# Global attention: split rows stored once, the first rows of maxima sent from ScalarE's queue, projections spread, tails by ScalarE and GpSimd, first local input early

## The chip, the cores and the metric

The kernel runs on one core of one Trainium2 chip. The metric is the device time of one execution in microseconds; lower is better. The kernel before took 2326.94 us in the median of three runs (2325.54 to 2329.14). Engine names in the profile: PE is TensorE (PEld its weight loads), DVE is VectorE, ACT is ScalarE, POOL is GpSimd, SP is SyncE, which here only issues DMAs (SPq is its queue).

## The reference

The input x is 1 x 2048 x 128 in fp32. It is normalised once (xn), and two things are computed from xn and added to x:

```python
xn = _layernorm(x)
x = x + attn(xn, Wq, bq, Wk, bk, Wv, bv, Wo, bo, U, V) + ffn_stack(xn, ...)

# attn: 16 heads of 8 numbers (V and U are 8 x 8), full softmax over 2048 keys
zq, zk, zv = q @ V, k @ V, v @ V
att = softmax(einsum('bhqr,bhkr->bhqk', zq, zk) / sqrt(8))
y = einsum('bhqk,bhkr->bhqr', att, zv) @ U.T ; return y @ Wo.T + bo

# ffn_stack: 6 layers, 16 heads of 64, windows of 32 tokens that look one window back
for i in range(6):
    x = local_attention_layer(shift_tokens(x)) + x     # q, k normalised, rotary tables
    x = ffn_layer(shift_tokens(x)) + x                 # layernorm, gated gelu
```

## The kernel before, in words

The program has two parts that run one after the other: the global attention (class `GlobalAttention`, about 0 to 697 us) and the six local layers (class `LocalStack`, from 697 us to the end). The second needs nothing of the first but xn, transposed, which lies in `xa`.

**Global attention.** A score needs more precision than one pass of the multiplier has, so queries and keys are split in a head (hi, the number rounded to the multiplier's format) and a tail (lo, what is left), and a score is the sum of three products: hi*hi, lo*hi, hi*lo. This is laid out along the contraction: a head's stack of queries has 8 rows each of hi, lo, hi, its stack of keys 8 rows each of hi, hi, lo, and row 24 (`ROWS`) holds a one on the keys' side and, on the queries' side, minus the maximum of the query's scores. Each stack stands twice in SBUF, on partitions 0 to 24 and 64 to 88, and matmuls use the two copies in turn (`half`, line 235). Two buffers of each stack alternate between heads (`qs[h % 2]`, `ks[h % 2]`).

For head 0 the stacks are computed directly (`first_stack`, line 145). For the others, `project` (line 202) computes 512 columns of all heads' queries or keys, ACT writes the head (line 209), DVE the tail (line 210), and `store_rows` (line 220) writes three pieces of 8 rows per head into a DRAM tensor `rows` of 25 rows per head. `load_stack` (line 228) later loads a head's 25 rows, with one DMA for each copy of each stack, in the middle of the head before.

The work of a head is four steps: "M" (`max_step`, line 241) computes 128 queries by 1024 keys on PE and reduces them to a maximum on DVE, 64 of them per head; "T" (`finish_max`, line 258) transposes the four maxima of a 512-query block, ACT negates them (`nm`, line 263) and two DMAs put them as row 24 into both copies of the query stack (line 266); "E" (`exp_step`, line 268) computes keys by queries again, with the maximum now subtracted by row 24, and ACT takes the exponential, 64 per head; "V" (`value_step`, line 277) multiplies by the values. The order is written out by hand in `STEPS` (line 59): a round has 8 M, 1 T, 16 E and 8 V, E runs 26 and V 17 steps behind. T comes after a round's second M; the first E that needs this T's maxima is the eleventh E of the round, right after the fifth M. `load_stack` for the next head stands at the head's 21st M. Before this, the steps M 0 to 2 carry the rest of `first_stack`, M 3 to 10 the eight projections and stores, M 11 to 14 the values (lines 370 to 377). From the 100th M on, each round also takes one step of `first_weights` of the local layers (line 482), which loads and splits the first layer's weights.

The order on each engine and in each DMA queue is the program's, under `manual_schedule`, except in the first stretch (lines 315 to 347), where only POOL's order is fixed. All DMAs of the program go through SP's queue. A DMA takes the next of eight completion semaphores and waits at its issue until the DMA before it on that semaphore has landed.

**Local layers.** 48 steps of 256 tokens run as a software pipeline: `ORDER` (line 390) lists all operations of a round with a lag each, and round n runs operation o for step n - lag (line 1097). What the change touches: `xh` and `xl` (lines 562, 565) split the input in head and tail, `tabq` and `tabk` (549, 552) load rotary tables, `tk` (555) scales them on ACT; `k` (588) projects keys, `k2` and `k1` (602, 597) multiply them by the tables on DVE, `ka` (608) adds on POOL. `xl` also clears the three `vbd` tiles on POOL in its first call (lines 570 to 573); `buffers` (519) clears `kbd` on DVE.

Of the kernel before, what the change touches and what calls it, by code (L numbers as in the profile page):

```python
# [8 lines left out]
F32 = mybir.dt.float32  # L9
F32R = mybir.dt.float32r  # L10
AF = mybir.ActivationFunctionType
ALU = mybir.AluOpType
# [4 lines left out]
T = 2048  # L17
# [44 lines left out]
class GlobalAttention:  # L62
# [139 lines left out]
    def project(self, n, b):  # L202
        nc = self.nc
        cols = bass.ts(b, 512)
        zh, zl = self.zsp[n] = [self.zs.tile([128, 512], F32R, tag=n + a, name=f"{n}_{a}") for a in "hl"]
        bz = self.bz[:, "qk".index(n) : "qk".index(n) + 1]
        ps = self.ps_st.tile([128, 512], F32, tag="st", name="ps_z")
        nc.tensor.matmul(ps, self.prod[n], self.xn_T[:, cols], start=True, stop=True)
        nc.scalar.activation(zh, ps, AF.Identity, bias=bz)
        nc.vector.scalar_tensor_tensor(zl, ps, bz, zh.bitcast(F32), ALU.add, ALU.subtract)  # L210

    def values_in(self, b):
        nc = self.nc
# [6 lines left out]
    def store_rows(self, n, b):  # L220

        cols = bass.ts(b, 512)
        for j, part in enumerate((0, 1, 0) if n == "q" else (0, 0, 1)):
            self.nc.sync.dma_start(
                out=self.rows[n][:, 8 * j : 8 * j + 8, cols], in_=self.zsp[n][part].bitcast(F32)
            )

    def load_stack(self, n, h):
        st = (self.qs if n == "q" else self.ks)[h % 2]
        for r in range(2):  # L230
            self.nc.sync.dma_start(
                out=st[64 * r : 64 * r + self.ROWS + 1, :].bitcast(F32), in_=self.rows[n][h]
            )

    def half(self, h):

# [21 lines left out]
    def finish_max(self, h, qb):  # L258
        nc = self.nc
        mt = self.ps_st.tile([128, 512], F32, tag="st", name="mt")  # L260
        nc.tensor.transpose(mt[0:4, 0:128], self.m, self.c["ident"])
        nm = self.sm.tile([4, 128], F32R, tag="nm", name="nm")
        nc.scalar.activation(nm, mt[0:4, 0:128], AF.Copy, scale=-1.0)
        for r in range(2):
            row = self.qs[h % 2][64 * r + self.ROWS : 64 * r + self.ROWS + 1, bass.ts(qb, 512)]
            nc.sync.dma_start(out=row.rearrange("o (a b) -> o a b", a=4).bitcast(F32), in_=nm.bitcast(F32))

    def exp_step(self, h, qb, kb):
        nc = self.nc
# [40 lines left out]
    def run(self):  # L310
        nc = self.nc
        self.zsp, self.mrow, self.pts, self.yp = {}, {}, {}, {}
        self.turns = 0
        self.rows = {n: self.dz.tile([NH, self.ROWS + 1, T], F32, name=f"rows_{n}") for n in "qk"}
        with self.tc.manual_schedule(engines={mybir.EngineType.Pool}):
            self.y = self.ps_y.tile([128, 512], F32, name="y")
            nc.vector.memset(self.y, 0.0)
            for b in range(2):
                self.norm(b)
            ones = self.w.tile([128, 256], F32, name="ones")  # L320
            nc.gpsimd.memset(ones, 1.0)
            zeros = self.w.tile([128, 256], F32, name="zeros")
            nc.gpsimd.memset(zeros, 0.0)
            self.qs = [self.stk.tile([128, T], F32R, name=f"qs{i}") for i in range(2)]
            self.ks = [self.stk.tile([128, T], F32R, name=f"ks{i}") for i in range(2)]
            for a in (self.qs[1], self.ks[1]):
                nc.gpsimd.memset(a.bitcast(F32), 0.0)
            self.zv = self.zp.tile([128, 16, NH, 9], F32, name="zv")

            for n, v in (("q", zeros), ("k", ones)):  # L330
                row = self.rows[n][:, self.ROWS, :]
# [12 lines left out]
            nc.gpsimd.memset(self.zv[:, :, :, 8:9], 1.0)  # L344
            for b in range(4):
                self.layer_input(b)
            self.output_bias()
        with self.tc.manual_schedule():
            self.steps()

    def steps(self):

        count = {"M": 0, "T": -1, "E": -26, "V": -17}
        size = {"M": 8, "T": 1, "E": 16, "V": 8}
        while count["V"] < 4 * 8 * NH:
            if count["M"] > 100:
                next(self.side, None)
            for o in STEPS:
                n = count[o]
                count[o] += 1  # L360
                qb, i = divmod(n, size[o])
                if not 0 <= qb < 4 * NH:
                    continue
                h, qb = divmod(qb, 4)
                if o == "M":
                    if (qb, i) == (2, 4) and h + 1 < NH:
                        self.load_stack("k", h + 1)
                        self.load_stack("q", h + 1)
                    self.max_step(h, 4 * qb + i // 2, i % 2)
                    if n < 3:  # L370
                        self.first_stack("q", n + 1)
                    elif n < 11:
                        z, b = "qk"[n % 2], (n - 3) // 2
                        self.project(z, b)
                        self.store_rows(z, b)
                    elif n < 15:
                        self.values_in(n - 11)
                elif o == "T":
                    self.finish_max(h, qb)
                    if qb == 3 and h:  # L380
                        self.sum_parts(h - 1)
                elif o == "E":
                    self.exp_step(h, qb, i)
                else:
                    self.value_step(h, qb, *divmod(i, 2))
                    if i == 7:
                        self.finish_exp(h, qb)


ORDER = """  # L390
    S.2@3 oh.2@4 pp.0@3 ptk@2 q2.3@2 k.0@1 O.3@4 tk@1 rk@2 wo.2@4 q1.3@2 sub.1@3 wt.qkv.1@2 wd.qkv.0@0 PT.0@3 ot.3@4
# [14 lines left out]
class LocalStack:  # L406
# [15 lines left out]
    def __init__(self, tc, ctx, io, const, xa, yd, out):  # L422
        self.tc, self.nc, self.io, self.c = tc, tc.nc, io, const
        self.xa, self.yd, self.out = xa, yd, out
        self.wl = {}
        self.pj = self.pT = None
        self.st = {}
        self.pw = ctx.enter_context(tc.tile_pool(name="b_w", bufs=1))
        self.pr = ctx.enter_context(tc.tile_pool(name="b_raw", bufs=1))
        self.free = {"raw": [0, 1], "pj": [0, 1, 2], "pt": [0, 1]}  # L430
        self.users = {}

# [49 lines left out]
    def first_weights(self):  # L482
        self.vectors(0)
        for kind, i in (("wo", 0), ("wo", 1), ("w2", 0)):
            self.w_whole((kind, 0, i), f"{kind}{i}", self.w_src(0, kind, i))
            yield
        for kind, i in [("qkv", g) for g in range(NG)] + [("w1", 0)]:
            self.w_load((kind, 0, i), self.w_src(0, kind, i))
            yield
            self.w_head((kind, 0, i), f"{kind}{i}")  # L490
            yield
            self.w_tail((kind, 0, i), f"{kind}{i}")
            yield

    def next_weights(step):
        def method(self, L, s, kind, i=0):
# [22 lines left out]
    def buffers(self, ctx):  # L519
# [16 lines left out]
        for t in self.kbd:  # L536
            for j in range(2):
                nc.vector.memset(t[64 * j : 64 * j + 64, :, :, 1 - j, :], 0.0)
        self.vturn = 0

    def tile(self, key, shape, bufs=1, dt=F32):
        self.st[key] = self.pb.tile(shape, dt, tag=key[0], name=key[0], bufs=bufs)
        return self.st[key]

    def vec(self, L, i):
# [19 lines left out]
    def xl(self, L, s):  # L565
        xh = self.st["xhead", L, s]
        self.nc.gpsimd.tensor_tensor(
            self.tile(("xtail", L, s), [128, TS], 2, F32R), self.xa[:, s * TS : (s + 1) * TS], xh.bitcast(F32), ALU.subtract
        )
        if (L, s) == (0, 0):  # L570
            for t in self.vbd:
                for j in range(2):
                    self.nc.gpsimd.memset(t[64 * j : 64 * j + 64, :, 1 - j, :], 0.0)


    def qk(self, L, s, g, t):
# [513 lines left out]
    def run(self):  # L1090
# [147 lines left out]
```

## Time and profile before

| what | us |
|---|---|
| median of 3 runs | 2326.94 |
| the profiled execution, its time | 2331.27 |
| its span, first to last instruction | 2329.2 |
| DVE's last step before local work (L256) | 680.19 |
| one round of global attention (between L256s) | 9.95 |
| PE busy / DVE busy / ACT busy in the span | 2200.6 / 2031.9 / 1725.1 |
| PE busy / DVE busy / ACT busy from 100 to 150 us | 50.00 / 48.10 / 46.45 |

The profile shows one execution. For each engine a row gives busy time; a group of instructions gives the source line, the engine, the operation, what is written from what, the count, the busy time, the mean time of one in ns, and the idle time of the engine before them with what ended it. The clock that PE was granted is shown as a share of the full one, and the DMA share is the mean busy share of the core's 16 DMA engines.

### The profile page before, as it was taken

To read this page: it belongs to the slowest core of one execution; us is meant where nothing else is said; L and a number is where in the kernel's file an instruction comes from. 1 tells how busy PE (TensorE), PEld (TensorE's weight loads), DVE (VectorE), ACT (ScalarE), POOL (GpSimd) and SP (SyncE) were. 2 spreads that over 40 slices of the span, in tenths; PEclk is the share of its full clock that TensorE was granted. 3 is DMA by queue.
4 is the path that set the end of the run, shared out by engine and by line. 5 is a ranking of instruction groups with operands and counts; after the bars stand their busy time and mean duration, and the time that the engine had idled before them with its cause. 6 is when DMAs were issued, how large, how long until landed. Compare 5 with 4: busy or idle time off the path is not lost.

```text
span 2329.2 us, 69662 instructions
## 1 busy us (share of the span) xinstructions
PE 2200.6 (94%) x27556; PEld 1612.0 (69%) x27556; DVE 2031.9 (87%) x3181; ACT 1725.1 (74%) x3333; POOL 1326.6 (57%) x1216
## 2 busy tenths in 40 slices
PE   6999999999996999999999999999899999999987
PEld 3444444444445888888888888888788878888875
DVE  7999999999975899888888888888799889898885
ACT  4999999999984667777677767676577767777654
POOL 2000100000006788878798778877698778878782
PEclk9999999999999999999999999999999999999998
DMA  4112121111115777877778878787687868777773
GB/s 140 52 60 80 62 69 62 53 63 53 62 47 158 211 215 218 224 223 202 215 220 221 226 205 218 205 225 210 176 229 214 217 189 230 219 216 217 205 214 82
DMA packets 295079, 384.69 MB, mean 165 GB/s; under 512 B 37256, under 2 KB 227464, under 8 KB 293256
## 3 DMA queue, kind: packets, MB, share of 16 engines
q1 hardware_dynamic: 294756, 380.25, 58.2%
q8 instruction: 220, 3.60, 0.7%
q14 instruction: 103, 0.84, 0.1%
HBM read 195.29 MB, written 77.59 MB: 117 GB/s over the span
## 4 chain that ended last, share of the span: by engine, by line
PE 57%; DMA 18%; SPq 9%; DVE 6%; POOL 4%; issue 3%; ACT 3%; POOLq 0%; DVEq 0%; ACTq 0%
PE y L282 11%; PE st L272 9%; PE s L248 6%; PE S L799 6%; DMA rd<-rkt 5%; DMA ur<-t2q 5%; PE ps_o L857 4%; PE ps_q L583 4%; PE ps_n L696 3%; SPq L787 3%; PE ps_wo L885 3%; PE pt_p L835 3%; DMA rbt<-rd 2%; SPq L636 2%; PE ps_v L659 2%
## 5 line engine op out<-in xcount | busy, mean ns | idle before, releaser
L251 DVE TENSOR_REDUCE m<-s 128x1 f32<-128x1024 f32 x512 | 602.2, 1219 | 30.7 <-PE s L248 24.0
L274 ACT ACTIVATE p<-st 128x512 f32<-128x512 f32 x1024 | 542.3, 598 | 44.0 <-PE st L272 13.7
L302 POOL TENSOR_TENSOR z<-z 72x512 f32<-72x512 f32 x15 | 19.2, 1281 | 590.0 <-DMA z<-yp 590.0
L640 POOL TENSOR_TENSOR t1q<-t1q,ur 128x512 f32<-128x512 f32 x192 | 244.7, 1285 | 158.9 <-DMA ur<-t2q 119.2
L282 PE MATMUL y<-p,zv 128*9 128x256 f32 x4096 | 293.1, 381 | 1.5 <-ACT ysb L292 1.5
L248 PE MATMUL s<-ks,qs 64*128 64x512 f32 x1024 | 280.3, 446 | 3.4 <-DVE m L251 1.9
L272 PE MATMUL st<-qs,ks 64*128 64x512 f32 x1024 | 273.0, 434 | 3.8 <-DMA qs<-nm 3.8
L819 POOL TENSOR_TENSOR P<-P,m 128x512 f32<-128x512 f32 x192 | 201.1, 1047 | 103.4 <-DVE m L815 102.8
L610 POOL TENSOR_TENSOR keys<-keys,t2k 128x512 f32<-128x512 f32 x192 | 247.9, 1291 | 5.8 <-DVE keys L599 5.4
L779 POOL TENSOR_TENSOR keys<-keys,rbt 128x512 f32<-128x512 f32 x192 | 243.7, 1294 | 7.2 <-DMA rbt<-rd 6.9
L857 PE MATMUL ps_o<-vbd,PTt 128*32 128x128 f32 x6144 | 210.4, 277 | 16.0 <-DMA vbd<-vd 14.1
L799 PE MATMUL S<-kbd,t1q 128*32 128x128 f32 x6144 | 211.7, 276 | 5.3 <-DMA kbd<-keys 4.5
L272 PEld LDWEIGHTS st<-qs,ks 64*128 64x128 f32 x1024 | 139.8, 184 | 110.5 <-ACT p L274 87.7
L823 POOL TENSOR_TENSOR P<-P,r 128x512 f32<-128x512 f32 x192 | 203.3, 1059 | 7.2
L624 DVE SCALAR_TENSOR_TENSOR t2q<-ps_q,vec,tabq 128x512 f32<-128x512 f32 x192 | 143.0, 745 | 73.7 <-DMA ur<-t2q 56.9
L799 PEld LDWEIGHTS S<-kbd,t1q 128*32 128x32 f32 x6144 | 174.0, 111 | 39.7 <-issue 12.6
L857 PEld LDWEIGHTS ps_o<-vbd,PTt 128*32 128x32 f32 x6144 | 157.8, 110 | 62.9 <-issue 38.5
L885 PE MATMUL ps_wo<-OT,w 128*128 128x256 f32 x768 | 198.7, 382 | 0.7 <-ACT OT L877 0.7
L644 ACT ACTIVATE sq<-ps_k 128x512 f32<-128x512 f32 x192 | 114.1, 595 | 109.3 <-PE ps_k L583 106.7
L248 PEld LDWEIGHTS s<-ks,qs 64*128 64x128 f32 x1024 | 120.9, 184 | 95.7 <-issue 82.3
L282 PEld LDWEIGHTS y<-p,zv 128*9 128x9 f32 x4096 | 74.4, 89 | 148.4 <-issue 96.2
L827 ACT ACTIVATE P<-P 128x512 f32<-128x512 f32 x192 | 121.6, 634 | 64.6 <-POOL P L823 63.8
(201 smaller groups left out, 5825.8 us busy)
## 6 DMA issues: line engine op xcount, KB each, us to landing
vbd<-vd SPq DMA_DIRECT2D x384, 256.0 KB
kbd<-keys SPq DMA_DIRECT2D x768, 72.0 KB
ur<-t2q SPq DMA_DIRECT2D x384, 128.0 KB
vd<-vn SPq DMA_DIRECT2D x96, 512.0 KB
rbt<-rd SPq DMA_DIRECT2D x192, 128.0 KB
tabk<-in_rope SPq DMA_DIRECT2D x48, 384.0 KB
yp<-ysb SPq DMA_DIRECT2D x64, 256.0 KB
tabq<-in_rope SPq DMA_DIRECT2D x48, 256.0 KB
```

The lines of the kernel that those rows point to most:

```text
L248: nc.tensor.matmul(s[:, j, :], q[:, bass.ts(qt, 128)], k[:, bass.ts(2 * hf + j, 512)], start=True, stop=True)
L251: nc.vector.tensor_reduce(self.mrow[h, qt // 4][:, qt % 4, hf : hf + 1], s.rearrange("p a b -> p (a b)"), AX.X, ALU.max)
L272: nc.tensor.matmul(st, k[:, bass.ts(kb, 128)], q[:, bass.ts(qb, 512)], start=True, stop=True)
L274: nc.scalar.activation(p, st, AF.Exp, scale=float(1.0 / 8.0**0.5))
L282: self.nc.tensor.matmul(self.y[32 * c : 32 * c + 9, cols], self.zv[:, kb, h, :], self.pts[h, qb, kb][:, cols], start=(j == 0 and half == 0 ...
L610: self.nc.gpsimd.tensor_tensor(t, t, self.st["t2k", L, s, g], ALU.add)
L640: self.nc.gpsimd.tensor_tensor(t, t, self.st["ur", L, s, g // 2][:, g % 2], ALU.add)
L779: self.nc.gpsimd.tensor_tensor(t, t, bmid(self.st["rbt", L, s][:, g, :], 2), ALU.mult)
L799: self.nc.tensor.matmul(S[32 * w : 32 * w + 32, 4 * i + 2 * p : 4 * i + 2 * p + 2, :], q[:, p, 32 * W : 32 * W + 32], kbd[:, p, :, 32 * W ...
L823: self.nc.gpsimd.tensor_tensor(P4, P4, bc(self.st["r", L, s][:, 0:2, g, :], 64), ALU.mult)
L857: self.nc.tensor.matmul(ps[32 * w : 32 * w + 32, i, p, :, :], PT[:, i, p, 32 * w : 32 * w + 32], vbd[:, w, :, c : c + 64], start=True, sto ...
L885: self.nc.tensor.matmul(self.st["acc", L, s], w[:, 2 * (g % 2) + c, :], o[:, c, :], start=(g == 0 and c == 0), stop=(g == 3 and c == 1),)
```

## The change

- `store_rows` stores each part once: `rows` has 17 rows per head, [lo, hi, row of zeros] for queries and [hi, lo, row of ones] for keys. `load_stack` builds the 25 rows of a stack from two pieces: 16 and 9 rows for queries, 8 and 17 rows for keys. So 8 DMAs load a head in place of 4.
- In `project` ACT writes the sum in fp32 once more (`z`), and POOL subtracts the head from it; DVE's line 210 is gone.
- The first six projections stay at M 3 to 8, two steps of values come at M 9 and 10, the last two projections at M 11 and 12, the last values at M 13 and 14. Keys come ahead of queries as before.
- For head 0 the two DMAs of `nm` are issued by ACT's queue, for the other heads by SP's.
- The clearing of `qs[1]` and `ks[1]` on POOL stands behind the copies into `xa`.
- `tabq`, `tabk`, `xh`, `tk`, `xl` of the first local step run as the last five steps of `first_weights`, one per round of global attention, and are left out where they stood; their tiles have a pool of their own that exists from the start. `vbd` is cleared in `buffers`.

```diff
     def project(self, n, b):
-        nc.vector.scalar_tensor_tensor(zl, ps, bz, zh.bitcast(F32), ALU.add, ALU.subtract)
+        z = self.zs.tile([128, 512], F32, tag="ft", name="z")
+        nc.scalar.activation(z, ps, AF.Identity, bias=bz)
+        nc.gpsimd.tensor_tensor(zl, z, zh.bitcast(F32), ALU.subtract)
...
     def store_rows(self, n, b):
-        for j, part in enumerate((0, 1, 0) if n == "q" else (0, 0, 1)):
-            self.nc.sync.dma_start(
-                out=self.rows[n][:, 8 * j : 8 * j + 8, cols], in_=self.zsp[n][part].bitcast(F32)
-            )
+        for part in range(2):
+            at = 8 * (1 - part if n == "q" else part)
+            self.nc.sync.dma_start(out=self.rows[n][:, at : at + 8, cols], in_=self.zsp[n][part].bitcast(F32))
 
     def load_stack(self, n, h):
-        st = (self.qs if n == "q" else self.ks)[h % 2]
+        st, rows = (self.qs if n == "q" else self.ks)[h % 2], self.rows[n][h]
         for r in range(2):
-            self.nc.sync.dma_start(
-                out=st[64 * r : 64 * r + self.ROWS + 1, :].bitcast(F32), in_=self.rows[n][h]
-            )
+            for to, size, src in ((0, 16, 0), (16, 9, 8)) if n == "q" else ((0, 8, 0), (8, 17, 0)):
+                lo = 64 * r + to
+                self.nc.sync.dma_start(out=st[lo : lo + size, :].bitcast(F32), in_=rows[src : src + size])
...
-            nc.sync.dma_start(out=row.rearrange("o (a b) -> o a b", a=4).bitcast(F32), in_=nm.bitcast(F32))
+            (nc.sync if h else nc.scalar).dma_start(out=row.rearrange("o (a b) -> o a b", a=4).bitcast(F32), in_=nm.bitcast(F32))
...
-        self.rows = {n: self.dz.tile([NH, self.ROWS + 1, T], F32, name=f"rows_{n}") for n in "qk"}
+        self.rows = {n: self.dz.tile([NH, 17, T], F32, name=f"rows_{n}") for n in "qk"}
...
-            for a in (self.qs[1], self.ks[1]):
-                nc.gpsimd.memset(a.bitcast(F32), 0.0)
...
             for b in range(4):
                 self.layer_input(b)
+            for a in (self.qs[1], self.ks[1]):
+                nc.gpsimd.memset(a.bitcast(F32), 0.0)
...
-                    elif n < 11:
-                        z, b = "qk"[n % 2], (n - 3) // 2
+                    elif n < 9 or n in (11, 12):
+                        i = n - 3 if n < 9 else n - 5
+                        z, b = "kq"[i % 2], i // 2
                         self.project(z, b)
                         self.store_rows(z, b)
                     elif n < 15:
-                        self.values_in(n - 11)
+                        self.values_in(n - 9 if n < 11 else n - 11)
...
+EARLY = ("tabq", "tabk", "xh", "tk", "xl")
...
+        self.pe = ctx.enter_context(tc.tile_pool(name="b_early", bufs=1, reuse_waits="tile"))
...
             self.w_tail((kind, 0, i), f"{kind}{i}")
             yield
+        for step in EARLY:
+            getattr(self, step)(0, 0)
+            yield
...
+        for t in self.vbd:
+            for j in range(2):
+                nc.gpsimd.memset(t[64 * j : 64 * j + 64, :, 1 - j, :], 0.0)
         self.vturn = 0
 
     def tile(self, key, shape, bufs=1, dt=F32):
-        self.st[key] = self.pb.tile(shape, dt, tag=key[0], name=key[0], bufs=bufs)
+        pool = self.pe if key[0] in ("tabq", "tabk", "tks", "xhead", "xtail") else self.pb
+        self.st[key] = pool.tile(shape, dt, tag=key[0], name=key[0], bufs=bufs)
...
-        if (L, s) == (0, 0):
-            for t in self.vbd:
-                for j in range(2):
-                    self.nc.gpsimd.memset(t[64 * j : 64 * j + 64, :, 1 - j, :], 0.0)
...
-                    if 0 <= n - lag < DEPTH * NS:
+                    if 0 <= n - lag < DEPTH * NS and (n > lag or step.__name__ not in EARLY):
                         step(*divmod(n - lag, NS), *args)
```

More of the change, by code (lines that the diff above doesn't have):

```diff
@@ L325, in run @@
             self.ks = [self.stk.tile([128, T], F32R, name=f"ks{i}") for i in range(2)]
-            for a in (self.qs[1], self.ks[1]):
-                nc.gpsimd.memset(a.bitcast(F32), 0.0)
             self.zv = self.zp.tile([128, 16, NH, 9], F32, name="zv")
             for n, v in (("q", zeros), ("k", ones)):
-                row = self.rows[n][:, self.ROWS, :]
+                row = self.rows[n][:, 16, :]
                 nc.sync.dma_start(out=row.rearrange("h (a b) -> h a b", a=8), in_=v)
```

## The prediction

> **What bounds the kernel now.** I read the page first (shares of the engines, 40 slices, groups), then the timeline at the three places that the change touches, the chain of waits there, and last the DMA traffic in small windows. In global attention DVE and ACT are nearly full beside a full PE:
>
> ```profile
> L251 DVE TENSOR_REDUCE m<-s 128x1 f32<-128x1024 f32 x512 | 602.2, 1219 | 30.7 <-PE s L248 24.0
> L274 ACT ACTIVATE p<-st 128x512 f32<-128x512 f32 x1024 | 542.3, 598 | 44.0 <-PE st L272 13.7
> ```
>
> A round is 9.95 us (from L256 to L256 on DVE's timeline), and PE is busy for all of 100 to 150 us. So what stops PE in a round is lost for good. Five rounds that hold one ACT cast of 0.84 us (L459) last 10.31: ACT has 0.84 - 0.36 = 0.48 us to spare in a round.
>
> The start (timeline): a POOL memset of a stack holds up a DVE instruction that elsewhere takes 0.15 us.
>
> ```profile
> 9.27 1.82 POOL L327 MEMSET ks<- 128x2048 f32 x1
> 9.29 1.83 DVE L177 TENSOR_SCALAR mu<-mu 128x4 f32<-128x4 f32 x1
> ```
>
> The first exponential (timeline): the maxima are ready at 46.6, their DMAs leave SP's queue at 51.7, behind stores, and PE stands 3.8 us.
>
> ```profile
> 46.33 0.25 ACT L263 ACTIVATE nm<-mt 4x128 fp32r<-4x128 f32 x1
> ...
> 51.71 1.47 SPq L266 DMA_DIRECT2D qs<-nm  x2
> ...
> 54.60 0.46 PE L272 MATMUL st<-qs,ks 64*128 64x512 f32 x1 [3.80 <-DMA qs<-nm]
> ```
>
> The join of the two parts (chain of waits): from 697.3 the chain is the table's load, its scaling, then DVE's first keys.
>
> ```profile
> 697.31 3.65 DMA tabk<-in_rope
> ...
> 703.50 0.69 DVE keys L599
> ```
>
> **The change part by part.** *Start.* DVE's four instructions at 9.29 to 11.2 would take about 0.6 us; the DMAs of x and the products of weights stay. I take -1.3 (0 to -2.0). Behind the copies into xa (about 25 to 29 us) the memsets meet DVE instructions that read PSUM; those kept 0.75 us beside POOL's copies at 22.4 to 25.6, so nothing; without that cover up to 1.8 each.
>
> *Warm-up.* DVE loses eight L210 of 0.75. ACT gets eight more of 0.69, POOL eight subtractions (1.28 by L640's group). Per projection PE then needs 1.48 (s at 30.19, 31.67, 33.15), ACT 1.38, POOL 1.28, DVE 1.22: PE sets the pace, where it was about 1.9. M 5 still starts at 35.1 (DVE), M 12 seven steps and one transpose of 0.4 later, at 45.9, its projection ends at 47.5, and there the first E may start. `nm` follows the transpose at 42.6 through ACT's queue: ready at 43.7, landed 2.76 later (51.71 to 54.47 now) at 46.5. So E starts at 47.5 where it was 54.6, and the round's end comes at 53.9 instead of 61.64, as the slow-clock stretch after the stop goes too: -7.6 (-4 if stores crowd `nm`, -9 at best). 16 stores of 256 KB instead of 24 lie behind this: at 338 GB/s, seen while the DMA share is 1, 12.4 us in place of 18.6.
>
> *nm from ACT.* The trace has no DMA on ACT's queue. Two on SP take 1.2 to 1.47 us; on ACT they may cost nothing or that. I take the row of the same transfer: 1.2 less 0.48 to spare is 0.7 in each of two rounds; in the round of the second T the second DMA also waits for the semaphore of a load of 17 rows, and ACT stands about 2 us. +3.4 (0 to +5).
>
> *Early input.* `tk` is two ACTIVATEs of 0.71 in one round: 1.42 - 0.48 = +0.9; `xh` (0.41) fits, POOL and SP have room for the rest.
>
> *Join.* Keys (L599) need the tables and the landing of the last `yp`, whose space they take. That is issued at 696.93; the one at 611.06 had moved its bytes 1.75 us later, so 698.7, against 703.50: -4.7, and -0.5 for the slow clock that follows PE's 4.1 us of idleness. -5.2 (-2.8 if `yp` lands late, -6.5). The memsets of `vbd` (5.9) go to POOL's idle time from 689.4; if they had to wait for the end of V, `ka` would be late by up to 2.
>
> *Loads of stacks.* SP issues 8 DMAs per head for 4, some 3.2 us in an idle queue that next has to send `yp` 6.7 us after the first load, and `nm` 8.7 us after it:
>
> ```profile
> 622.97 1.20 SPq L266 DMA_DIRECT2D qs<-nm  x2
> 624.23 0.80 SPq L231 DMA_DIRECT2D ks<-rows_k  x2
> 625.07 0.64 SPq L231 DMA_DIRECT2D qs<-rows_q  x2
> 630.96 0.34 SPq L295 DMA_DIRECT2D yp<-ysb  x1
> 632.92 1.23 SPq L266 DMA_DIRECT2D qs<-nm  x2
> ```
>
> The bytes stay the same, but look at what carries them. First row: `z` is loaded with 72 partitions; second: the loads of 25 rows.
>
> ```profile
> 646.20:646.40 0.20, 0.20 (x3) 0.00 (x0) 0.20 (x1) 0.20 (x2) 0.00 (x0) 1.00 0.82 292
> ...
> 628.50:630.50 2.00, 2.00 (x23) 0.94 (x25) 1.97 (x3) 1.86 (x5) 0.00 (x0) 1.00 0.31 131
> ```
>
> 0.31 of 16 engines is five, with four DMAs in flight: each uses five, and all the same five. 72 partitions reach some 0.75, twelve; the 128 of `yp` reach 1.0. Five divides 25, twelve 72, sixteen 128: the largest number up to 16 that divides the count fits all rows. 17 has only 1. Five engines at 131 GB/s are 26.2 each, 0.313 us per row of 8 KB. The bounds for a piece of 17 rows are thus one engine and the five of 25 rows. With five the busiest engine carries 16 rows per head, under today's 20, and nothing is lost. With one, the first engine carries 1+17+1+17 rows of keys and 1+1+1+1 of queries: 40. I take one.
>
> [...]
>
> Now the clock of a head, from the issue of its first load (624.23): packets move at +1.07 and today end at +8.1, 0.8 of start and 20 rows of 0.313. With 40 rows they end at +14.4. Behind them in the same queue stand the engine's sixteenth of `yp` (0.7) and its part of `nm`: +15.2. Today PE's first E with these maxima starts at +11.65 and waits for nothing:
>
> ```profile
> 632.32 0.27 PE L261 MATMUL mt<-ident,m 128*4 128x128 f32 x1
> ...
> 635.52 0.84 PE L272 MATMUL st<-qs,ks 64*128 64x512 f32 x3
> ```
>
> So PE stands 3.5 us, and with it everything, as M, E and V follow in PE's order: 14 heads (1 to 14; head 0's `nm` has ACT's queue, head 15 loads nothing) x 3.5 = +49 (0 by the five-engine bound; 4.2 each, +59, if a lone engine starts slower). The next head's first M, at +16.8 plus this stop, finds its stacks.
>
> After the 3.8 us of idleness at 50.8 the clock fell to half:
>
> ```profile
> 55.00:56.00 1.00, 1.00 (x7) 0.77 (x5) 0.66 (x1) 0.60 (x1) 0.00 (x0) 0.67 1.01 326
> 56.00:57.00 1.00, 1.00 (x6) 0.93 (x5) 0.56 (x1) 0.00 (x0) 0.00 (x0) 0.50 0.96 344
> ```
>
> It stayed there for 3.4 us, as after the 4.1 us at 700. PE, the bound, loses half of such a stretch, 1.7; part of it may fall into the stop itself: 1.4 per head, +20 (0 to 24).
>
> Sum: -1.3 - 7.6 + 3.4 + 0.9 - 5.2 + 49 + 20 = +59. The profiled execution took 2331.27 (span 2329.2 and 2.1 around it), so 2390 for a profile like it; the median of the runs is 4.3 lower: 2326.9 + 59 = 2386. **Forecast: 2385 us.**
>
> **The rivals.** *One:* 17 rows do not pile up on an engine that `nm` needs, because they are split like 25 or later DMAs start at other engines. Then the loads cost nothing and 2326.9 - 9.8 = 2317. The point: up to 28 rows on the busiest engine (11.65 - 1.07 - 0.8 - 0.8 = 9.0 us) PE waits for nothing. For it: the eight packets of 8 and 16 rows are spread better than today. Against: four DMAs in a row now use the same five engines. Chance 0.10. *Two:* the pile is there, but the clock stays full, as the stop is just about one stretch of 3.4 us: 2386 - 20 = 2366. Against: 3.8 and 4.1 us were enough twice. Chance 0.20. *Three:* PE's stop is also short, since a lone engine may move a row faster than 0.313; at 0.27 a head loses 1.8 and little clock: 2326.9 - 9.8 + 25 = 2342. Chance 0.07. *That the change does not do what it says:* the queue of ACT saves nothing if the first E then waits for its own projection; this is in the 47.5 above.
>
> **How the numbers follow.** The forecast has 0.63; its own range is 2368 (2.9 and 0.8 per head) to 2404 (4.2 and 1.7). With the second rival and part of the third the range is 2352 to 2402. A measurement here tells 0.2%, 4.7 us, from no change. Slower by more: 0.63 + 0.20 + 0.07 = 0.90, less 0.02 for sums that end near zero; faster 0.10; same 0.02.
>
> **What would show it.** A PE group L274 with some 3.5 us waits for qs<-nm, 14 of them in one place of each head; a round in four that lasts 13 to 15 us; windows after the loads with a DMA share of 0.06 at 26 GB/s for over 9 us; clock digits under 9 from slice 2 to 11. If the share is 0.3 or more there, rival one holds. Apart from this: the first E near 46 us, L599's successor some 1.8 us after the last `yp` issue, ACT's second `nm` of head 0 waiting for ks<-rows_k. It is wrong if PE waits for the stacks at a head's first M instead, or if local rounds change their length.

## The result and the profile after

The changed kernel is slower: median 2454.44 us (2451.81 to 2465.22, 6 runs) against 2328.04 (2325.14 to 2338.33, 6 runs) for the kernel before on the same chip, ratio 1.0541 (95% interval 1.0513 to 1.0570). The profiled execution took 2453.93 us with a span of 2452.1. The predicted 2385 had the place and the direction right and about half of the size.

The page's groups of the kernel after (busy time, mean ns of one, then the idle time of the engine before them and what ended most of it):

```profile
L253 DVE TENSOR_REDUCE m<-s 128x1 f32<-128x1024 f32 x512 | 606.6, 1220 | 160.1 <-PE s L250 151.8
L276 ACT ACTIVATE p<-st 128x512 f32<-128x512 f32 x1024 | 543.3, 599 | 172.9 <-PE st L274 136.9
L274 PE MATMUL st<-qs,ks 64*128 64x512 f32 x1024 | 286.5, 451 | 102.5 <-DMA qs<-nm 95.2
```

The busy times of DVE and ACT are those of before, within 1%. What is new is idle time: 31 became 160 us before DVE's maxima, 44 became 173 before ACT's exponentials, 4 became 102 before PE's E. The list of waits (us in total, times, longest) names the one that the other two follow:

```profile
DVE m L253 <- PE s L250: 151.8, 130, 9.2
ACT p L276 <- PE st L274: 136.9, 109, 8.7
PE st L274 <- DMA qs<-nm: 95.2, 15, 9.0
```

One of the 15 is 0.17 us long, so 14 stops take 95 us, 6.8 each. One head on the timeline:

```profile
599.18 1.35 SPq L235 DMA_DIRECT2D ks<-rows_k  x4
600.58 1.41 SPq L235 DMA_DIRECT2D qs<-rows_q  x4
...
605.91 0.34 SPq L297 DMA_DIRECT2D yp<-ysb  x1
...
609.56 1.22 SPq L268 DMA_DIRECT2D qs<-nm  x2
...
617.33 0.76 PE L274 MATMUL st<-qs,ks 64*128 64x512 f32 x1 [6.47 <-DMA qs<-nm]
```

The maxima were computed at 607.85 and issued at 609.56, and PE got them at 617.33, 18.15 us after the head's first load was issued; 11.65 is when it would have been ready for them. The windows of the same stretch (length, busy time of each engine, then granted clock, DMA share, GB/s) show two phases:

```profile
600.00:602.00 2.00, 2.00 (x23) 0.80 (x15) 2.00 (x3) 1.87 (x5) 0.00 (x0) 1.00 0.51 131
602.00:604.00 2.00, 2.00 (x21) 0.90 (x17) 2.00 (x2) 1.78 (x5) 0.00 (x0) 1.00 0.67 111
...
610.00:612.00 2.00, 0.86 (x8) 0.38 (x4) 1.90 (x2) 1.85 (x4) 0.00 (x0) 1.00 0.07 26
612.00:614.00 2.00, 0.00 (x0) 0.00 (x0) 0.00 (x0) 0.00 (x0) 0.00 (x0) 1.00 0.06 25
...
618.00:620.00 2.00, 2.00 (x13) 0.63 (x12) 1.23 (x1) 0.60 (x1) 0.00 (x0) 0.50 0.00 0
```

From 608 on, when the next `yp` has landed, the share is 0.06 or 0.07 at 25 to 31 GB/s: one engine of sixteen, as predicted, here until 615.9. But before that eight to eleven engines (0.51 and 0.67 of sixteen) move no more than 111 to 131 GB/s together. The packets' records say the same: 67 of the head's 100 rows start in the first 5.2 us and take 0.69 in the median and up to 1.08 us, where a row took 0.309 before the change; after 605.5 the lone engine moves 33 rows at 0.313. And the half clock lasts longer than the 3.4 us that the forecast took from the kernel before: 6.8 or 10.2 us per stop, which begin while PE still stands (here 614.4 to 621.2, and PE starts at 617.33).

Rounds are closed by the step L258 of DVE. After head 0, three in four last about 9.95 us, one in four 17.7 to 21.3, and the excess of the 14 sums to 122.3 us, 8.7 per head.

### The profile page after: what moved, and what is told of

Its sections match the earlier page's. It is cut to its first block, busy times and chain, and to the rows that moved or that the text cites. A ratio compares the mean times of both kernels' runs of the same rounds, so it can differ in the third digit from the quotient of the medians.

```text
span 2452.1 us, 69726 instructions
## 1 busy us (share of the span) xinstructions
PE 2230.3 (91%) x27556; PEld 1619.3 (66%) x27556; DVE 2029.5 (83%) x3173; ACT 1727.9 (70%) x3341; POOL 1336.9 (55%) x1224
## 4 chain that ended last, share of the span: by engine, by line
PE 60%; DMA 20%; SPq 8%; DVE 4%; ACT 3%; issue 3%; POOL 3%; ACTq 0%; POOLq 0%; DVEq 0%
PE y L284 10%; PE st L274 8%; PE s L250 6%; PE S L808 6%; DMA ur<-t2q 5%; DMA qs<-nm 4%; PE ps_o L866 4%; DMA vbd<-vd 4%; PE ps_q L592 4%; PE ps_wo L894 4%; PE ps_n L705 3%; PE pt_p L844 3%; SPq L796 3%; PE ps_v L668 3%; DMA kbd<-keys 2%
## 5 line engine op out<-in xcount | busy, mean ns | idle before, releaser
L274 PE MATMUL st<-qs,ks 64*128 64x512 f32 x1024 | 286.5, 451 | 102.5 <-DMA qs<-nm 95.2
L284 PE MATMUL y<-p,zv 128*9 128x256 f32 x4096 | 305.8, 395 | 2.0 <-ACT ysb L294 2.0
L250 PE MATMUL s<-ks,qs 64*128 64x512 f32 x1024 | 292.3, 463 | 1.7 <-ACT ks L156 1.7
L250 PEld LDWEIGHTS s<-ks,qs 64*128 64x128 f32 x1024 | 127.0, 194 | 94.8 <-issue 83.9
L872 DVE TENSOR_TENSOR Ot<-ps_o,rsum 128x512 f32<-128x512 f32 x192 | 130.9, 682 | 44.9 <-PE ps_o L866 44.7
```

Source lines behind the costliest of these rows:

```text
L250: nc.tensor.matmul(s[:, j, :], q[:, bass.ts(qt, 128)], k[:, bass.ts(2 * hf + j, 512)], start=True, stop=True)
L274: nc.tensor.matmul(st, k[:, bass.ts(kb, 128)], q[:, bass.ts(qb, 512)], start=True, stop=True)
L284: self.nc.tensor.matmul(self.y[32 * c : 32 * c + 9, cols], self.zv[:, kb, h, :], self.pts[h, qb, kb][:, cols], start=(j == 0 and half == 0 ...
```

## The experiments

The kernel before ran beside each group of experiments on the same chip. Its median there was 2334 to 2340, not 2328, so ratios are compared, and inside the traces the places on the timeline.

### 1. The 17 rows cut in two

```diff
-            for to, size, src in ... else ((0, 8, 0), (8, 17, 0)):
+            for to, size, src in ... else ((0, 8, 0), (8, 8, 0), (16, 9, 8)):
```

> The changed kernel with the keys' 17 rows loaded as 8 and 9 rows (12 load DMAs per head for 8); nothing else differs. In the changed kernel's trace PE waits 6.5 to 9 us in one place of each of 14 heads, and with the half clock after it a head loses 8.7 us. Theory (17 rows pile up on one engine and the maxima queue behind them): no engine now has more than a few rows, the waits for qs<-nm go, and with them 14 x 8.7 = 122 us and some 8 us of ACT's wait in head 0: 2454 - 130 = 2324, so 2318 to 2328, no slower than the kernel before. Rival (what costs is the number of load DMAs, or the semaphores they share, and not the 17): 12 DMAs are no better than 8, 2450 or more.

Measured: ratio 1.0045 (1.0021 to 1.0069). Nearly all of the loss is gone with nothing but a different cut of the same bytes, so the piece of 17 rows is the cause, and the number of load DMAs is not (it grew from 8 to 10: six for keys and four for queries; the 12 of the expectation is miscounted). But it is not quite "no slower": the list of waits still has

```profile
PE st L274 <- DMA qs<-nm: 11.3, 11, 2.2
```

and a head still loses 1.0 us. By the prediction's estimate of the engines of a piece none has more than ten rows now, yet a head's loads last 9.1 to 10.3 us from the first packet's start to the last one's end in all heads but the first (7.1), longer than the 7 of the old layout with twenty rows on each of five engines (a share of 0.31). A count of rows alone can't explain that.

### 2. The rows as before, the rest of the change kept

```diff
-            for to, size, src in ((0, 16, 0), (16, 9, 8)) if n == "q" else ((0, 8, 0), (8, 17, 0)):
-                lo = 64 * r + to
-                self.nc.sync.dma_start(out=st[lo : lo + size, :].bitcast(F32), in_=rows[src : src + size])
+            self.nc.sync.dma_start(
+                out=st[64 * r : 64 * r + self.ROWS + 1, :].bitcast(F32), in_=self.rows[n][h])
```

(and `store_rows` and `rows` as before the change)

> The changed kernel with the storing and loading of rows as before the change (25 rows stored, 4 loads of 25 rows per head); all else of the change stays. Theory: the other parts are worth about -8 (start -10, join -5.5, ACT's queue +3.4, early input and the last rounds +4), so 2320, between 2316 and 2325; and within 3 us of the kernel with the 17 rows cut in two. Rival (the loss comes from the spread projections or from ACT's queue): still above 2400.

Measured: 0.9993 (0.9971 to 1.0015). The loss is gone, but the gain of 8 us isn't there either; 1.6 is the middle of the interval. Its trace against that of before: the first round's end comes 7.2 us earlier; head 0's other three rounds take 4.6 more (ACT issues the maxima: 1.1 in each of two rounds, 2.4 in the one with the loads); some 1 us more in the other rounds; 2.3 us more between the last maxima and the last E (below); the first keys 4.5 us sooner after the last E. That sums to -3.7; what is left lies in the local layers, which took from 1623.5 to 1636.5 us after the first keys in the eleven traces of the whole kernel, whatever the version. Single executions can't settle a few us there; only the ratios can.

### 3. Only the rows changed

The kernel before with `store_rows`, `load_stack` and `rows` of the change.

> The kernel before with only the storing and loading of rows changed (17 rows stored, pieces 8 + 17 and 16 + 9). Theory: each of 15 heads loses 8.7 us (head 0 too, as its maxima also go through SP's queue): +131; fewer stores stand ahead of the first maxima: -2 to -6. 2328 + 131 - 4 = 2455, between 2435 and 2465. Rival (the split rows alone are harmless): under 2340.

Measured: 1.0549 (1.0519 to 1.0580), as much as the whole change. So the split rows alone make the loss, now in 15 heads, since head 0's maxima go through SP's queue too: 8.8 us per head.

### 4. Loads by themselves

A kernel that computes no attention: groups of load DMAs of 8 KB rows, each group after the last has landed and been read.

```diff
+        for to, size, at, pitch, step, *q in pieces:
+            nc.sync.dma_start(out=t[to : to + (size - 1) * step + 1 : step, :],
+                              in_=src[pitch][at : at + size, 0:2048])
```

> No attention is computed: the kernel stores zeros as output and makes groups of load DMAs of 8 KB rows, each group alone and after the last has landed. In the changed kernel the lone engine's rows took 0.313 us when it was alone, but 0.5 to 1.0 while up to 16 engines were loading. 17 rows in one DMA: one packet at a time, 17 x 0.313 = 5.3 us. Two such DMAs together: 10.6 us if both have the same engine, 5.3 if not. Why rows take longer in company, three theories. Place (engines that write neighbouring partitions share a way in): 16 rows to 16 neighbouring partitions take 0.5 us or more each, to every fourth or eighth partition about 0.32, whatever the source. Source (engines that read rows 8 KB apart collide): a source with 12 KB from row to row brings them to 0.32, the partitions do nothing. Sum (some 110 to 130 GB/s for all engines together): neither helps, a row takes 1.0 us with 16 engines, 0.5 with 8, and 0.31 with 5. The eight loads of a head as in the changed kernel: 15 to 16 us from first to last packet; with the 17 cut in 8 and 9: 5 to 8; the four loads of 25 rows: 6 to 7.

Measured, from the packets' records (each group twice; us from the first packet's start to the last one's end, ns of a row in the median):

| group | us | ns per row |
|---|---|---|
| 17 rows | 6.2, 5.2 | 309, one at a time |
| two times 17 rows (two halves of the stack) | 11.3, 11.6 | 309, one at a time |
| 16 rows, neighbouring partitions | 0.62, 0.57 | 463, 342 |
| 16 rows, every 4th / every 8th partition | 0.59, 0.75 / 0.62, 0.78 | 399, 420 / 455, 399 |
| 16 rows, 12 KB apart in the source | 0.74, 0.77 | 484, 418 |
| a head's key pieces, as changed | 12.2, 12.2 | 309 |
| a head's query pieces, as changed | 3.4, 3.1 | 621, 513 |
| all eight pieces of a head | 15.8, 15.8 | 533, 559 |
| the same, 12 KB apart in the source | 15.4, 15.3 | 455, 467 |
| all ten with the keys cut in 8 and 9 | 9.4, 9.3 | 924, 909 |

The windows of that kernel over the two 17s, over the eight pieces (two windows), and over the cut pieces (DVE, POOL, clock, DMA share, GB/s):

```profile
41.00:51.00 10.00, 0.00 (x0) 0.00 (x0) 1.00 0.06 26
73.00:78.00 5.00, 0.00 (x0) 0.00 (x0) 1.00 0.56 97
78.00:88.00 10.00, 0.15 (x1) 0.00 (x0) 1.00 0.06 26
106.00:111.00 5.00, 0.00 (x0) 0.00 (x0) 1.00 0.62 84
```

Two DMAs of 17 rows take twice the time of one (11.3 and 11.6 us against 6.2 and 5.2), at 0.06 of the engines and 26 GB/s: both use the same engine. That one engine takes all 17 rows was the prediction's estimate from the shares seen with 25, 72 and 128 rows; this run shows it for 17. The 15.8 us of the eight pieces is the head of the changed kernel, with no compute around it, and it is not 40 x 0.313 = 12.5. Keys alone are 12.2: the queries, only four rows of the first engine, add 3.6 us. Why company slows a row this run did not tell: in a single DMA of 16 rows neither the partitions nor the source made a clear difference, against the theories of place and of source as they were written. The cut pieces, with 62% of the engines busy at 84 GB/s, are the extreme of it: 9.4 us where 5 to 8 were expected. The four loads of 25 rows began while the cut queries were still landing, so their time can't be read; theirs were the only rows of that stretch back at 309 ns.

### 5. The queries' loads out of the way

```diff
-                    if (qb, i) == (2, 4) and h + 1 < NH:
-                        self.load_stack("k", h + 1)
-                        self.load_stack("q", h + 1)
+                    if (qb, i) == (1, 6) and h + 1 < NH:
+                        self.load_stack("q", h + 1)
+                    if (qb, i) == (2, 4) and h + 1 < NH:
+                        self.load_stack("k", h + 1)
```

> The changed kernel with the loads of the next head's queries issued 6 M steps (7.5 us) ahead of those of the keys; the pieces are the same. In the groups of loads measured by themselves the four key pieces took 12.2 us, all eight together 15.8. Theory (the lone engine's rows are slowed while others load): the pile now ends 1.07 + 12.2 = 13.3 us after the first key load is issued, yp's share and the maxima bring E to +14.7 where it is due at +11.65: PE waits 3.1 us per head for 6.5 to 9 now, with the clock 4.5 to 6 for 8.7: 2454 - 14 x 3.5 - 3 = 2402, between 2385 and 2415. Rival (company does not matter, only the lone engine's 40 rows do): 4 rows or 1.25 us less of wait, so about 7.4 per head, 2436. If the maxima of the round before now wait behind the queries: over 2454.

Measured: 2403.71 us, ratio 1.0300 (1.0276 to 1.0324). The list of waits:

```profile
PE st L274 <- DMA qs<-nm: 49.5, 15, 5.0
```

3.5 us of stop per head and 5.1 us lost with the clock, and the key pieces last 12.1 to 13.5 us in all heads but the first. Almost the same pile (36 rows instead of 40), same queue behind it: without the company of the queries it costs what the prediction had given for the whole (3.5 and 4.9). For 36 rows, though, the prediction's own reckoning gives a stop of 2.2 us, so that the two numbers meet is partly luck.

### 6. A smaller pile

```diff
-            for to, size, src in ... else ((0, 8, 0), (8, 17, 0)):
+            for to, size, src in ... else ((0, 8, 0), (8, 8, 0), (16, 9, 8)) if r else ((0, 8, 0), (8, 17, 0)):
```

> The changed kernel with the keys' 17 rows cut in 8 and 9 for one half of the stack only: the first engine carries 25 rows (1 + 17 + 1 + 1 + 1 and 4 of the queries) where it carried 40. By the prediction's reckoning (0.313 us per row whatever else runs; PE waits for nothing up to 28 rows) no head waits, and the time is that of the kernel cut in both halves or less: 2325 to 2345. Theory (rows cost 0.7 to 0.9 us while other engines load): the first 8 rows take some 6.5 us, 17 more 5.3, and E comes at 1.07 + 11.8 + 0.7 + 0.75 = 14.3 instead of 11.65: 2.7 us of waiting per head, 3.5 to 4.5 with the clock, 14 x 4 = 56: 2330 + 56 = 2386, between 2370 and 2400.

Measured: 2392.80 us, ratio 1.0251 (1.0228 to 1.0275). The list of waits:

```profile
PE st L274 <- DMA qs<-nm: 35.0, 14, 4.0
```

25 rows on the first engine, three fewer than the point from which the prediction reckoned a wait, and PE stops 2.5 us per head. The reckoning of 0.313 us for every row is refuted; the loads of a head last 10.5 to 12.0 us.

### 7. Why company is slow

Again loads alone, six equal DMAs in a row to six tiles:

```diff
+    ("near16", (0, 16, 0, 1)), ("step4", (0, 16, 0, 4)), ("step8", (0, 16, 0, 8)),
+    ("near16_pitch", (0, 16, 1, 1)), ("step8_pitch", (0, 16, 1, 8)),
+    ("near8", (0, 8, 0, 1)), ("step4_8", (0, 8, 0, 4)), ("five25", (0, 25, 0, 1)),
```

(first partition, rows, source with 8 or 12 KB from row to row, step of the partitions)

> No attention is computed: the kernel stores zeros as output and runs groups of six equal load DMAs, to six tiles, of 16 rows (or 8, or 25) of 8 KB. In a single DMA of 16 rows neither a spread of the partitions nor another row distance of the source made a clear difference (0.6 to 0.78 us in all). Theory 1 (place: four neighbouring partitions share one way in of about 26 GB/s, which a short burst does not fill): six times 16 rows to partitions 0 to 15 take 96 / 4 x 0.313 = 7.5 us, to every fourth or eighth partition (8 ways) 3.75; six times 8 neighbouring rows 7.5 too (2 ways), to every fourth partition 1.9. Theory 2 (a limit of some 120 GB/s on all such loads): 6.5 us near and spread alike, 3.3 for 8 rows. Theory 3 (source): the groups with 12 KB from row to row are faster than those with 8 KB. 25 rows on five engines: 30 rows each, 9.4 us in all theories.

The windows over the first six groups, in that order, second time round (DVE, POOL, clock, DMA share, GB/s):

```profile
77.60:83.90 6.30, 0.69 (x4) 0.00 (x0) 1.00 0.97 124
87.00:90.90 3.90, 0.70 (x5) 0.00 (x0) 1.00 0.65 202
93.20:97.60 4.40, 0.68 (x4) 0.00 (x0) 1.00 0.62 177
99.50:106.20 6.70, 0.69 (x4) 0.00 (x0) 1.00 0.86 113
108.90:113.00 4.10, 0.69 (x4) 0.00 (x0) 1.00 0.65 192
114.80:120.90 6.10, 0.69 (x4) 0.00 (x0) 1.00 0.49 64
```

The step decides and the source doesn't: six times 16 rows take 6.3 to 7.1 us on neighbouring partitions and 3.7 to 4.4 on every fourth or eighth, with 8 or with 12 KB between rows. On neighbouring partitions a row takes 1.20 us in the median (0.80 in one of the six groups: three kinds, twice each), four times 0.30: this fits four engines that write four neighbouring partitions and take turns on one way in. That is the author's reading of the times; a way itself stands in no trace. Eight neighbouring rows get 64 GB/s at 0.49 of the engines (two ways by this reading); 25 rows in one DMA, on five engines, keep their 0.309, which would fit five consecutive rows to each, though no run shows which rows an engine has. The sixteen rows of a single DMA in the run before had passed in 0.6 to 0.8 us, so a short burst does not show it.

Six times 8 rows on every fourth partition took 4.2 and 4.7 us instead of the expected 1.9. SP's queue shows why: it issues a DMA with spread partitions more slowly. Six DMAs of 16 neighbouring rows, of 16 rows on every eighth partition, of 8 neighbouring rows, and of 8 rows on every fourth partition (start, time on the queue):

```profile
98.56 2.62 SPq L58 DMA_DIRECT2D d<-src  x6
107.68 3.64 SPq L58 DMA_DIRECT2D d<-src  x6
113.94 2.06 SPq L58 DMA_DIRECT2D d<-src  x6
123.05 4.18 SPq L58 DMA_DIRECT2D d<-src  x6
```

The spread groups thus lasted about as long as their issue. Their 3.7 to 4.4 us do not show the eight ways from which 3.75 had been expected, and no other run does; what they show is that spread rows keep up with a DMA every 0.63 us, where neighbouring ones need 1.1. Rows on every fourth partition were not at 0.31 either: those 8 took 0.44 and 0.47 us in the median, which stays open.

### 8. The rows of the stacks apart

Rows on every second partition of a half (0, 2, ..., 48), the first head's matrices likewise; in between there are zeros.

```diff
-                lo = 64 * r + to
-                self.nc.sync.dma_start(out=st[lo : lo + size, :].bitcast(F32), in_=rows[src : src + size])
+                lo = 64 * r + 2 * to
+                self.nc.sync.dma_start(out=st[lo : lo + 2 * size - 1 : 2, :].bitcast(F32), in_=rows[src : src + size])
```

With the 17 rows cut as in experiment 1:

> The kernel with the keys' 17 rows cut in 8 and 9 (1.0045 of the kernel before; PE still waited some 1 us in 11 of the heads that the trace caught, the loads of a head lasted 9.3 us), now with the rows of a stack on every second partition (0, 2, 4 to 48 of each half, the matrices of the first head likewise); the sums are the same, since the partitions between hold zeros. In the loads by themselves, engines that wrote four neighbouring partitions shared 26 GB/s. Theory: 16 rows then have 8 ways for 4 and 8 rows 4 for 2, a head's loads end within 6 to 7 us of their first packet, PE's waits for qs<-nm go, some 14 us with them: ratio 0.998 to 0.9995. Rival (the place matters only in the loads by themselves, here the ten DMAs cost their issue): 1.0045 as before.

Measured: 0.9969 (0.9957 to 0.9980). No wait of PE for `nm` is left in the heads. The windows from some 1.6 us after the issue of a head's first load, first of the kernel with the cut alone, then with the rows apart (PE, PEld, DVE, ACT, POOL, clock, DMA share, GB/s):

```profile
597.00:599.00 2.00, 2.00 (x18) 0.72 (x16) 2.00 (x2) 1.79 (x5) 0.00 (x0) 1.00 0.60 115
599.00:601.00 2.00, 2.00 (x27) 0.94 (x29) 2.00 (x3) 1.87 (x4) 0.00 (x0) 1.00 0.96 131
```

```profile
580.00:582.00 2.00, 2.00 (x17) 0.72 (x15) 2.00 (x3) 1.78 (x5) 0.00 (x0) 1.00 0.22 70
582.00:584.00 2.00, 2.00 (x27) 0.91 (x29) 2.00 (x3) 1.87 (x4) 0.00 (x0) 1.00 0.35 107
```

107 GB/s now need 0.35 of the engines where 115 and 131 needed 0.60 and 0.96: a row takes 0.35 to 0.48 us in the median of a head instead of 0.87 to 0.94 (0.45 in the first). The same ten DMAs last 6.7 to 8.3 us instead of 9.1 to 10.3, although SP now takes 6.8 us or more to issue them instead of some 4.3, as in experiment 7. They now last about as long as their issue.

With the pile left as in the change:

> The changed kernel with nothing but the rows on every second partition; 17 rows in one DMA stay, 40 rows on the first engine stay. Theory: what is left is the pile without most of the sharing, 40 x 0.313 = 12.5 us and up to 1 more: E at 1.07 + 12.5 to 13.5 + 0.7 + 0.75 = 15.0 to 16.0 for 11.65, PE waits 3.4 to 4.4 per head for 6.8, and loses 4.9 to 6.2 with the clock for 8.7: 14 x 3.1 = 44 and some 3 of ACT's wait in head 0 less than the changed kernel's 1.054, so 1.03 to 1.038. Rival (the slowing has another cause): 1.054.

Measured: 1.0467 (1.0454 to 1.0481), a third to a half of the step that was expected. Of its waits the list has

```profile
PE st L274 <- DMA qs<-nm: 79.9, 14, 6.9
```

5.7 us per head instead of 6.8; the loads last 13.8 to 14.9 us instead of 15.2 to 17.3. So the place explains some 1.4 us of the 3.2 that the pile lasts longer than 40 x 0.313, and PE gains only 1.1 of them, since the first packet now moves 1.42 us after its issue instead of 1.07. With every second partition two engines may still share a way (by the reading of experiment 7), and the first rows of a queue take longer (0.79 and 0.68 us for the first two of the two 17s in experiment 4). How the rest divides between these two stays open.

### 9. Versions that beat both kernels

The old rows, with ACT's queue for the kernel's very first maxima only and `xh`, `xl` off the list of early steps:

```diff
-            (nc.sync if h else nc.scalar).dma_start(
+            (nc.sync if h or qb else nc.scalar).dma_start(
-EARLY = ("tabq", "tabk", "xh", "tk", "xl")
+EARLY = ("tabq", "tabk", "tk")
```

> The changed kernel with the rows stored and loaded as before the change, ACT's queue used only for the very first maxima of the kernel, and the first local input (xhead, xtail) not made early, so that the 18 local products of PE stay out of the last global rounds; tables early as in the change. By the trace of the kernel with the old rows: start -7.2 against the kernel before, ACT's queue in later rounds was +4.6 and is now 0, the 18 products cost PE 2.3 there and now fill the wait at the join, the join itself -4 to -5.5. Sum -9 to -12: ratio 0.9955 to 0.996 to the kernel before on the same chip. Rival (the end of the local part absorbs what the global part gains): 0.999 to 1.001.

Measured: 2320.72 us, 0.9944 (0.9923 to 0.9965). Head 0's later rounds are back at 9.95. But the 18 local products did not go: their first is still ahead of the last T, with `xh` off the list,

```profile
675.12 0.39 PE L592 MATMUL ps_k<-xhead,wh 128*128 128x256 f32 x1
```

so that part of the expectation failed; the list alone isn't what let them in. In this version the tiles of `xh` and `xl` still lie in the pool that exists from the start, which may be the reason; a version without it wasn't tried.

The rows stored once, cut and apart, with the same two edits:

> Rows stored once (17), the keys' pieces cut in 8 and 9, rows on every second partition, ACT's queue for the very first maxima only, the first local input not made early. Against the version with the old rows (0.9944 of the kernel before) it has 16 stores for 24 ahead of the first blocks, worth 0 to 3 us, and ten load DMAs for four, worth nothing if they end in time: 0.993 to 0.9945. Rival (more wide loads delay the maxima now and then): 0.996 or more.

Measured: 2323.22 us, 0.9934 (0.9913 to 0.9955). The two intervals overlap: storing each part once can't be told from storing it twice, but both are faster than the kernel before, by 0.35% at the least by their intervals.

## Why the prediction was wrong, step by step

The two profiled executions differ by 122.97 us in span. Cut at the same places on the timeline:

| step | predicted | measured |
|---|---|---|
| start and warm-up, to the first round's end | -8.9 | -10.05 |
| head 0's other rounds (`nm` from ACT) | +3.4 | +11.7 |
| PE's stops in 14 heads | +49 | +95 |
| what these heads lose beyond the stop | +20 | +27.3 |
| early input, other rounds | +0.9 | +2.5 |
| last maxima to last E | 0 | +2.2 |
| last E to first keys | -5.2 | -4.3 |
| local layers | 0 | -1.4 |
| sum | +59 | +123 |

*The step that failed.* "Five engines at 131 GB/s are 26.2 each, 0.313 us per row of 8 KB", used for all 40 rows of the first engine. The mechanism was right: 17 rows on one engine (an estimate then, 0.06 of the engines in experiment 4), the engine's part of `nm` queued behind, 14 stops in that place. The size was off because 0.313 is the row's time with 25 rows on five engines (0.309 in experiment 7) or when one engine works alone. The new pieces of 8, 9 and 16 rows go to neighbouring partitions with eight to eleven engines at work (0.51 and 0.67 of the sixteen), and while they ran, the first engine moved 7 rows in 5.2 us. The pile ended 16.7 us after the first load's issue for a predicted 14.4; another 0.7 was left out between the moment that `nm`'s last packet moves (616.6) and PE's start (617.33); it is 0.71 to 0.73 in all 14 heads. 2.3 + 0.7 is the 3.0 that a stop was too short in the head shown (6.5 for 3.5). How much of the 2.3 is the place is only in part shown: rows on every second partition took 1.4 off the pile (experiment 8). Experiment 5, with less company, gave the predicted stop, but with four rows fewer; experiment 6, under the predicted point of 28 rows, gave a stop all the same. The bounds were drawn for the number of engines and not for the time of a row; the four DMAs of 25 rows had only ever shown rows that take 0.309.

*The clock.* Predicted 1.4 per head from stretches of 3.4 us; 1.95 measured. The loss beyond the stop, as the excess of the heads' rounds less PE's waits, against the stop (for experiment 1 the stops of all 14 heads, of which the list names 11):

| | stop, us per head | lost beyond it |
|---|---|---|
| cut in two (1) | 1.0 | 0.1 |
| half cut (6) | 2.5 | 1.0 |
| queries early (5) | 3.5 | 1.5 |
| pile apart (8) | 5.7 | 2.1 |
| the change | 6.8 | 1.9 |

At the predicted stop of 3.5 the predicted 1.4 was about right. Longer stops get longer stretches at half clock (4.1 us per head in experiment 5, 7.8 in the change), of which a part falls into the stop itself. Rival two, a full clock, is out, and so are one and three: the pile is there, and a lone row takes 0.313, not 0.27.

*Its sums and readings.* The range's upper end of 2404 doesn't follow from its 4.2 and 1.7 per head, which give 2400. The row shown for 72 partitions has a share of 0.82 and not 0.75; with its neighbours (0.70 and 0.77) the mean is 0.76, so twelve engines still fit best. Neither moves the forecast.

*Head 0.* Predicted: 0.7 in each of two rounds and "ACT stands about 2 us" for the load's semaphore in the third. The two took 1.15 and 1.11. The third on the timeline of the kernel after, ACT's queue and ACT:

```profile
54.02 7.44 ACTq L268 DMA_DIRECT2D qs<-nm  x2
61.51 2.07 ACT L276 ACTIVATE p<-st 128x512 f32<-128x512 f32 x4 [7.52 <-DMA ks<-rows_k]
```

ACT's second DMA waits for the semaphore of a piece of 17 rows on the slowed engine, and all exponentials stand behind it: 9.4 us of that round. The wait was named and its place right; its length hung on the landing of that piece. With the old rows (experiment 2) the same round lost 2.4, with the rows cut and apart 1.1.

*Start and warm-up.* Right within 1.2 us: M steps every 1.49 us instead of 1.7 to 2.1, the first E at 45.95 (47.5 predicted). The difference arose at the start: DVE's first maximum begins at 23.46 instead of 26.02, 2.6 us earlier, where 1.3 (0 to 2.0) had been predicted.

*The join.* Lines of the kernel after:

```profile
825.55 0.34 SPq L297 DMA_DIRECT2D yp<-ysb  x1
826.06 0.69 DVE L614 TENSOR_TENSOR t2k<-ps_k,tks 128x512 f32<-128x512 f32 x1 [14.21 <-ACT sq L653]
827.85 0.69 DVE L608 TENSOR_TENSOR keys<-ps_k,tks 128x512 f32<-128x512 f32 x1 [1.10 <-DMA yp<-ysb]
```

The first keys come 2.3 us after the issue of the last `yp` (predicted 1.8) and wait for its landing, as said. What the prediction did not see: PE now does 18 products of the first local round (from 807.10) ahead of the last T and V. Before, they filled PE's wait at the join (they ran from 697.25); now they cost 2.2 us in a round in which PE is the bound. Early work was not free on an engine without room.

So of the gains outside the loads, predicted at 14 us against 4 of costs, 14 arrived, but the costs there grew to 16 as the change stands. In the best versions ACT's cost is gone and 13 to 15 us are left in the ratio.

## What to carry to other kernels

Before a DMA's rows are recounted, work out on which engines the new count lands (25 rows had 0.31 of the sixteen here, 17 rows 0.06), how many rows the busiest of them carries with the other DMAs of that moment, and which small transfer stands behind it in the same queue. Then ask which partitions those engines write at the same time: a row of 8 KB took 0.31 us in DMAs of 25 rows and 1.20 when 16 or 8 engines wrote neighbouring partitions (experiment 7). And before a wait is put on a compute engine's queue, ask which transfers share its semaphore: ACT stood 7.5 us here until a load of keys had landed.

## What the runs showed of the hardware that was not expected

- Engines that write neighbouring partitions slow each other: 1.20 us per row of 8 KB with 16 or 8 engines on neighbouring partitions, 0.40 to 0.47 on every fourth or eighth, 0.31 alone (experiments 4 and 7). A single DMA of 16 rows (0.6 to 0.8 us) does not show it.
- Spread partitions cost time at the issue: six DMAs of 16 rows kept SP's queue 3.6 us instead of 2.6, six of 8 rows 4.2 instead of 2.1 (experiment 7).
- More engines can be slower: ten DMAs over up to 16 engines took 9.1 to 10.3 us (experiment 1) for the 100 rows that four DMAs on five engines had moved in 7 before the change.
- PE's clock is at half for 6.8 or 10.2 us with stops of 6 to 9 us (the change), for 3.4 or 6.8 with stops of about 3.5 (3 to 5, experiment 5); part of it falls into the stop.
- PE starts 0.71 to 0.73 us after the last packet of the maxima it waits for (the change, 14 heads).
- Two DMAs issued by ACT cost its round 1.1 us (the change, head 0), where 0.48 of slack had been seen.
